# Layer norms cut into pieces, the two cell gates in one product, and the expert bias added on GpSimd, in a two-layer gated cross-attention kernel

## The chip, the cores and the metric

The kernel runs on one NeuronCore of one Trainium2 chip. A core has TensorE (PE) for matrix products, VectorE (DVE) and ScalarE (ACT) for work along rows, GpSimd (POOL) for other elementwise work, and SyncE (SP), which here only issues DMAs. [...] The metric is the device time of one execution in microseconds, the median of several runs.

## The reference

Eight sequences of 512 tokens with 256 features each (`x`) pass through two layers, with a context of the same shape. All numbers are float32. Cut to what matters:

```python
# layer 0: a gated linear cell (8 heads of 32) over the context
q = layernorm(x);  k = v = ctx
ifg = concat([q, k, v], axis=-1)              # 768 features; k and v are the same tensor
ig = ifg @ igate_w.T + igate_b;  fg = ifg @ fgate_w.T + fgate_b
cs = cumsum(log_sigmoid(fg));  log_D = causal(cs_s - cs_t + ig_t)
C = (q @ k.T / sqrt(32)) * exp(log_D - max(log_D))
h = (C / (max(|sum C|, exp(-max log_D)) + 1e-6)) @ v
x = x + tanh(g_xattn[0]) * layernorm(h) * ln_scale
# layer 0: self-attention with 32 heads of 8, then 8 experts of fixed token blocks
xn = layernorm(layernorm(x)) * ln_g + ln_b
o = softmax(q @ k.T / sqrt(8)) @ v @ wo + layernorm(x)
y = gelu(o_block @ w1[e] + b1[e]) @ w2[e] + b2[e]     # 256 tokens per expert and sequence
x = x + tanh(g_ffn[0]) * y
# layer 1: cross-attention with 16 heads of 16 and a key mask
x = x + tanh(g_xattn[1]) * (softmax(mask(layernorm(x) Wq . ctx Wk)) @ (ctx Wv) @ Wo + bo)
# layer 1: product-key memory of 4096 experts, top 8 of 8 heads
x = x + tanh(g_ffn[1]) * memory(layernorm(x))
```

Since `k` and `v` of the cell are the same context, a gate's weights on `k` and on `v` meet the same factors.

## The kernel before

The kernel has three stages. The first holds the cell, both attentions, the experts and most of the first product of the memory; a second folds the memory's batch norm into its keys; a third finds the top keys and adds up the memory's rows. The change touches the first stage only, so the other two are told no further.

Tokens lie on the 128 partitions in `NC` = 4 blocks, with 256 features along the row, where a layer norm is done; products need the features on the partitions, and `to_features` (L243) gets there by eight transposes on TensorE and two copies.

The first stage is written as a planner. An outer loop (L937) walks the softmax attentions, 24 jobs of 16 steps, with two half-ticks per step. In each half-tick it issues two score products for the row maxima of one job (`maxima`, L325) and two for the exponentials of the job before (`exponentials`, L353); after them come the maximum on VectorE (L333) and the exponential on ScalarE (L361), and in every second half-tick the products with the values (L376). Scores have two PSUM buffers for both kinds together, so the next pair of a kind waits until the last one was read. Then `beside` (L915) hands out side work for a credit of 1.3 or 2.4 units. Side work comes in five lanes, generators that issue a few instructions and then yield:

- a number is the cost of TensorE work just issued, taken from the credit;
- `("wait", t)` puts the lane to sleep until the planner's clock `now` has gone on by `t`. The clock moves at the end of a half-tick alone, by 2.6 units (`RETURN`) or by the work issued, if that is more;
- `("rest", event)` waits for another lane, and `("take", True)` for the one accumulator bank `ac` of PSUM.

The lane `before` (L843) runs `cell` (L440) and `queries` (L602) for each sequence `m`, `behind` runs `experts` (L645), `operands` (L712) and `values1`, `after` runs `leave` (L760), and `fill` runs `inner` (L798), products of the memory that fill what is left.

The order that comes out of this binds TensorE alone (`ORDERED`, L31). The other engines' queues are ordered by a scheduler, which takes instructions as it finds them ready, the earlier written first among equals, and which also sets the waits. DMAs in `load`, `load_context` and `load_expert` go through GpSimd's queue, nearly all others through SyncE's.

What the change touches:

- `layernorm` (L83): four statistics (L90), four aggregates (L92), the variance's power of -1/2 on GpSimd (L93, L94), four normalizations (L96). It is called for six norms per sequence: `qn` and `hk` in the cell, two in `queries`, one each in `operands` and `leave`. All its instructions are issued at once; the caller then waits, mostly 6.5 units.
- The gates of the cell (L457 to L472): for each of two gates six products of 8 output rows by 512 tokens (L463), two with the query's features and four with the context's, into `ac`, and an addition of the bias (L469).
- The end of the cell (L593 to L599): the norm of `hk`, its scale `lns` on VectorE (L594), and the addition to the freshly loaded `X` on GpSimd (L598).
- The experts (L668 to L707): after eight blocks of the first product (L674) and the Gelu (L685), the second product starts with a product of a row of ones with the bias row `b2e` (L689) and goes on with sixteen products (L696); the result, times `tanh(g)`, is added to `X` (L702). `load_expert` (L428) fetches `w1e`, `w2e` and `b2e` of the next expert, with one buffer each.

## Time and profile before

| what | value |
|---|---|
| median of 3 runs | 4510.04 us (4505.13 to 4513.51) |
| profiled execution | 4499.43 us, of which the span from first to last instruction 4497.7 us |
| mean granted TensorE clock | 0.915 |
| products of the gates (L463) | 192 records, 592 ns each (two records per product) |
| products of the bias (L689) | 32 records, 620 ns each (two per product) |
| norm: statistics, aggregate, normalization | 192 each; 410, 154 and 408 ns |
| norm: power on GpSimd (L93, L94) | 48 each; 227 and 1040 ns |
| scale of `hk` on VectorE (L594) | 8, 1221 ns |
| addition to `X` on GpSimd (L598) | 8, 2167 ns |
| `x2` on GpSimd (L656) | 32, 1219 ns |
| load of `b2e` | 16, 1 KB each, 1.7 us from issue to landing |

A record's duration is from its start to its modelled end; products overlap in TensorE's pipeline, so the spacing of two starts says what one costs. The profile names a line, an engine, an operation and its tiles; behind an arrow stands what ended the idle time ahead of it.

### The profile page before, as it was taken

To read this page: it belongs to the slowest core of one execution; us is meant where nothing else is said; L and a number is where in the kernel's file an instruction comes from. 1 tells how busy PE (TensorE), PEld (TensorE's weight loads), DVE (VectorE), ACT (ScalarE), POOL (GpSimd) and SP (SyncE) were. 2 spreads that over 40 slices of the span, in tenths; PEclk is the share of its full clock that TensorE was granted. 3 is DMA by queue.
4 is the path that set the end of the run, shared out by engine and by line. 5 is a ranking of instruction groups with operands and counts; after the bars stand their busy time and mean duration, and the time that the engine had idled before them with its cause. 6 is when DMAs were issued, how large, how long until landed. Compare 5 with 4: busy or idle time off the path is not lost.

```text
span 4497.7 us, 74502 instructions
## 1 busy us (share of the span) xinstructions
PE 3866.6 (86%) x30857; PEld 1939.2 (43%) x30857; DVE 2473.7 (55%) x5662; ACT 1586.7 (35%) x2035; POOL 563.0 (13%) x572
## 2 busy tenths in 40 slices
PE   6778797879988998998899898788997689999998
PEld 2222333433334333333334343233444366666667
DVE  3555534554454455455544534443200599999995
ACT  2124343334443543443344344442431122332331
POOL 3110101100011001001100100000000122222222
PEclk7679889999999999999999999998998689999999
DMA  3210112122213222222321231102345012222221
GB/s 95 46 38 25 39 43 64 50 60 84 64 51 96 79 60 71 86 60 74 80 84 60 74 110 37 44 23 62 102 134 119 25 67 91 88 86 89 91 89 42
DMA packets 191983, 312.73 MB, mean 70 GB/s; under 512 B 20430, under 2 KB 145902, under 8 KB 184238
## 3 DMA queue, kind: packets, MB, share of 16 engines
q1 hardware_dynamic: 173452, 239.98, 17.8%
q0 software_dynamic: 15520, 62.94, 5.0%
q10 hardware_dynamic: 2672, 5.04, 0.4%
q8 instruction: 243, 3.98, 0.4%
q14 instruction: 96, 0.79, 0.1%
HBM read 218.85 MB, written 88.24 MB: 68 GB/s over the span
## 4 chain that ended last, share of the span: by engine, by line
PE 62%; DVE 19%; DMA 3%; ACT 2%; issue 2%; POOL 1%; SPq 0%; DVEq 0%; POOLq 0%; ACTq 0%
PE sc L316 18%; PE acc L1272 9%; PE ps_hd L118 8%; DVE nm L333 7%; PE av L376 6%; PE ps_y L696 3%; PE ps_h L674 2%; PE ps_p L267 2%; PE ps_q L278 2%; PE ps_sim L1153 2%; PE cf L1254 1%; PE ps_hl L118 1%; DVE gs L1263 1%; DVE m L1241 1%; DVE m L1243 1%
## 5 line engine op out<-in xcount | busy, mean ns | idle before, releaser
L333 DVE TENSOR_REDUCE nm<-sc 128x2 f32<-128x1024 f32 x768 | 939.6, 1224 | 1114.0 <-PE sc L316 1112.3
L316 PE MATMUL sc<-ka,qa 32*128 32x512 f32 x3072 | 968.5, 688 | 284.3 <-DVE nm L333 256.2
L361 ACT ACTIVATE pr<-sc 128x1024 f32<-128x1024 f32 x768 | 785.1, 1023 | 1195.5 <-PE sc L316 1192.9
L316 PE MATMUL sc<-qa,ka 32*128 32x512 f32 x3072 | 925.5, 674 | 13.0 <-ACT pr L361 7.4
L316 PEld LDWEIGHTS sc<-ka,qa 32*128 32x128 f32 x3072 | 262.9, 195 | 716.9 <-DVE nm L333 501.4
L1272 PE MATMUL acc<-up_sb,gs 64*128 64x256 f32 x4096 | 495.3, 397 | 43.2 <-DVE gs L1263 43.2
L118 PE MATMUL ps_hd<-xT,dw 128*64 128x256 f32 x3584 | 435.0, 388 | 20.4 <-DVE pd L555 8.5
L1272 PEld LDWEIGHTS acc<-up_sb,gs 64*128 64x128 f32 x4096 | 409.0, 197 | 100.1 <-DVE gs L1263 45.3
L376 PE MATMUL av<-pr,v 128*32 128x512 f32 x3072 | 437.2, 643 | 5.5 <-ACT pr L361 5.5
L118 PEld LDWEIGHTS ps_hd<-xT,dw 128*64 128x64 f32 x3584 | 242.2, 138 | 253.9 <-issue 101.9
L1244 POOL TENSOR_TENSOR m<-m,chT 128x1024 f32<-128x1024 f32 x128 | 257.1, 2008 | 723.9 <-DVE m L1243 556.4
L316 PEld LDWEIGHTS sc<-qa,ka 32*128 32x128 f32 x3072 | 249.6, 192 | 63.8 <-issue 26.7
L814 ACT COPY hb<-ps_hd 128x512 f32<-128x512 f32 x224 | 131.0, 585 | 326.6 <-PE ps_hd L118 291.9
L376 PEld LDWEIGHTS av<-pr,v 128*32 128x32 f32 x3072 | 62.1, 111 | 320.9 <-issue 303.3
L528 ACT ACTIVATE pd<-mb,aT 128x512 f32<-128x512 f32 (+3 forms) x256 | 129.6, 553 | 176.0 <-PE cav L535 84.2
L520 POOL TENSOR_SCALAR_AFFINE_SELECT mb<-mb 128x256 f32<-128x256 f32 x128 | 52.1, 407 | 1111.4 <-ACT pd L528 520.5
L1254 PEld LDWEIGHTS cf<-m,m 64*64 64x64 f32 x8192 | 139.8, 142 | 91.6 <-issue 75.3
L1254 PE MATMUL cf<-m,m 64*64 64x64 f32 x8192 | 156.9, 229 | 23.4 <-DVE gs L1263 18.2
L1241 DVE TENSOR_TENSOR m<-chT,iota 128x1024 f32<-128x1024 f32 x128 | 170.6, 1332 | 2.0 <-ACT chT L1230 2.0
L555 DVE SCALAR_TENSOR_TENSOR pd<-csc,pd 128x512 f32<-128x512 f32 (+3 forms) x256 | 115.7, 485 | 92.0 <-PE csc L550 67.1
L1187 ACT ACT_TABLE_LOAD x28 | 35.9, 1283 | 360.8 <-DVE w L1186 341.9
L550 PE MATMUL csc<-qT,cT 32*128 32x256 f32 (+3 forms) x512 | 146.9, 554 | 17.1 <-DVE pd L555 13.2
(215 smaller groups left out, 4366.8 us busy)
## 6 DMA issues: line engine op xcount, KB each, us to landing
h_d<-hb SPq DMA_DIRECT2D x224, 256.0 KB
gs<-h_d SPq DMA_DIRECT2D x56, 1024.0 KB
dw<-in_down SPq DMA_DIRECT2D x112, 256.0 KB
w1e<-in_w POOLq DMA_DIRECT2D x16, 1024.0 KB, 5.4
w2e<-in_w POOLq DMA_DIRECT2D x16, 1024.0 KB, 6.5
mb<-nM_d SPq DMA_DIRECT2D x32, 512.0 KB
qk_d<-pk SPq DMA_DIRECT2D x64, 256.0 KB
ws<-in_w SPq DMA_DIRECT2D x56, 256.0 KB
```

The costliest lines, as they stand in the source:

```text
L118: nc.tensor.matmul(ps[64 * q : 64 * q + 64, :], dw[:, k, :], runs[:, :, q, :], start=(k == 0), stop=(k == NK - 1),)
L316: nc.tensor.matmul(sc[:, i, :], lhs[r : r + 32, g, c * P : (c + 1) * P], rhs[r : r + 32, g, :], start=True, stop=True,)
L333: nc.vector.tensor_reduce(self.nm[:, c, 2 * half : 2 * half + 2, g], sc, AX.X, ALU.max, negate=True)
L361: nc.scalar.activation(self.pr[jj], sc, AF.Exp)
L376: nc.tensor.matmul(self.av[32 * j : 32 * j + 32, :], self.va[:, c, h * (self.hd + 1) : h * (self.hd + 1) + 32], pr[j // 2][:, j % 2, :], s ...
L550: nc.tensor.matmul(sc[i][:, s0:], cT[r : r + 32, g, s0 : s0 + P], qT[r : r + 32, g, s0:], start=True, stop=True,)
L696: nc.tensor.matmul(py[:, c, :], hT[:, f, c * P : (c + 1) * P], w2e[:, f, :], start=False, stop=(f == NF - 1 and c == 1),)
L814: nc.scalar.copy(hb.rearrange("p n i t -> p i n t"), ps.rearrange("p i (n t) -> p i n t", n=2),)
L1241: nc.vector.tensor_tensor(m1, spread(0), grid, ALU.is_equal)
L1244: nc.gpsimd.tensor_tensor(m2, m2, spread(2), ALU.mult)
L1254: nc.tensor.matmul(cf[64 * q : 64 * q + 64, h, s, :], m2[rows, q, s, :], m1[rows, q, s, :], start=True, stop=True,)
L1272: nc.tensor.matmul(accs[n][q], gs[n % 2][rows, i, :], up_sb[rows, i, :], start=(i == 0), stop=(i == 63),)
```

## The change

Six edits, in the order of the code:

1. `layernorm` becomes a generator with four pieces. It yields after two statistics, after the power, and after each two normalizations, with waits of 1, 3, 1.5 and 1.5 units; callers use `yield from` and drop their own waits after it (in `queries` two, 5 and 6.5; in the cell, `operands` and `leave` 6.5 each). Its small tiles get tags by user.
2. At the start, the gates' weights are gathered in a tile `gwm` of 40 columns: one gate in columns 0 to 7, the other in 32 to 39, with the weights on `k` and `v` summed. Biases are loaded to the same rows. `gw_sb` and `m_f` move into the buffers of later tiles.
3. The cell's gates are one accumulation of four products with 40 output rows, from which both gates are read.
4. The scale of `hk` moves from VectorE to GpSimd, and the waits around the addition to `X` are changed from 6 and 2 units to one of 5 after it.
5. `b2e` is loaded broadcast to all partitions, scaled by `tanh(g)` on GpSimd, and added there to the expert's half of `X` before its products.
6. The expert's second product loses the bias product, and its sixteen products run with the token half outside and the feature block inside.

The diff, less the removed empty lines and the unchanged context:

```diff
...
     nc.sync.dma_start(tg, gates.partition_broadcast(P))
     nc.scalar.activation(tg, tg, AF.Tanh)
-    def layernorm(dst, src, keep=1):
-        st = small.tile([P, NC, 6], F32, name="ln_st")
-        mv = small.tile([P, NC, 2], F32, name="ln_mv", tag=f"ln_mv{keep}", bufs=keep + 1)
-        rs = small.tile([P, NC], F32, name="ln_rs", tag=f"ln_rs{keep}", bufs=keep + 1)
+    def layernorm(dst, src, user):
+        st = small.tile([P, NC, 6], F32, name="ln_st", tag=f"ln_st{user}", bufs=1)
+        mv = small.tile([P, NC, 2], F32, name="ln_mv", tag=f"ln_mv{user}", bufs=4 if user == "x" else 1)
+        rs = small.tile([P, NC], F32, name="ln_rs", tag=f"ln_rs{user}", bufs=4 if user == "x" else 1)
         for c in range(NC):
             nc.vector.bn_stats(st[:, c, :], src[:, c, :])
+            if c == 1:
+                yield ("wait", 1)
         for c in range(NC):
             nc.vector.bn_aggr(mv[:, c, :], st[:, c, :])
         nc.gpsimd.tensor_scalar(rs, mv[:, :, 1], EPS_LN, None, ALU.add)
         nc.gpsimd.tensor_tensor(rs, rs, mhalf.to_broadcast([P, NC]), ALU.pow)
+        yield ("wait", 3)
         for c in range(NC):
             nc.vector.tensor_scalar(
                 dst[:, c, :], src[:, c, :], mv[:, c, 0:1], rs[:, c : c + 1], ALU.subtract, ALU.mult
             )
+            if c % 2:
+                yield ("wait", 1.5)
         return mv, rs
...
         ps_m = ctx.enter_context(tc.tile_pool(name="ps_m", bufs=2, space=PSUM))
-        gw_sb = cst.tile([P, 6, 16], F32, name="gw_sb")
+        gw_sb = row.tile([P, 6, 16], F32, name="gw_sb", tag="cs")
         nc.sync.dma_start(gw_sb, gw.rearrange("(k p) n -> p k n", p=P))
-        gb_sb = cst.tile([8, 2], F32, name="gb_sb")
-        nc.sync.dma_start(gb_sb, gb)
+        gb_sb = cst.tile([40, 1], F32, name="gb_sb")
+        for i in range(2):
+            nc.sync.dma_start(gb_sb[32 * i : 32 * i + 8], gb[:, i : i + 1])
+        gwm = cst.tile([P, 4, 40], F32, name="gwm")
+        nc.gpsimd.memset(gwm, 0.0)
+        for i in range(2):
+            part = slice(8 * i, 8 * i + 8)
+            nc.vector.tensor_copy(gwm[:, 0:2, 32 * i : 32 * i + 8], gw_sb[:, 0:2, part])
+            nc.vector.tensor_tensor(
+                gwm[:, 2:4, 32 * i : 32 * i + 8], gw_sb[:, 2:4, part], gw_sb[:, 4:6, part], ALU.add
+            )
         class Weights:
...
         m_u8 = cst.tile([B * NC, P], U8, name="m_u8")
         nc.sync.dma_start(m_u8, mask)
-        m_f = cst.tile([B * NC, P], F32, name="m_f")
+        m_f = row.tile([B * NC, P], F32, name="m_f", tag="e")
         nc.vector.tensor_copy(m_f, m_u8)
         mp = ps_m.tile([P, S], F32, name="mp", tag="m")
         nc.tensor.transpose(mp[:, : B * NC], m_f, ident[: B * NC, : B * NC])
...
             nc.gpsimd.dma_start(w1e, w1[e].rearrange("(k p) f -> p k f", p=P))
             w2e = wmp.tile([P, NF, D], F32, name="w2e", tag="w2e")
             nc.gpsimd.dma_start(w2e, w2[e].rearrange("(f p) d -> p f d", p=P))
-            b2e = wmp.tile([1, D], F32, name="b2e", tag="b2e")
-            nc.gpsimd.dma_start(b2e, b2[e : e + 1])
+            b2e = wmp.tile([P, D], F32, name="b2e", tag="b2e")
+            nc.gpsimd.dma_start(b2e, b2[e].partition_broadcast(P))
             weights[n] = (e, w1e, w2e, b2e)
...
                     cx[b, c * P : (c + 1) * P].rearrange("p (h e) -> p h e", e=32),
                 )
             yield ("wait", 4)
-            layernorm(qn, qn)
-            yield ("wait", 6.5)
+            yield from layernorm(qn, qn, "q")
             qT = trp.tile([P, NK, S], F32, name="qT", tag="qT")
             yield from to_features(qT, qn)
+            yield ("take", True)
+            gp = ps_ac.tile([P, S], F32, name="gp", tag="ac")
+            for k in range(4):
+                if k:
+                    yield 0.9
+                nc.tensor.matmul(
+                    gp[:40], gwm[:, k, :], qT[:, k, :] if k < 2 else cT[:, k - 2, :],
+                    start=(k == 0), stop=(k == 3),
+                )
             gates = []
             for i in (1, 0):
-                yield ("take", True)
-                gp = ps_ac.tile([P, S], F32, name="gp", tag="ac")
-                for k in range(6):
-                    if k:
-                        yield 0.9
-                    nc.tensor.matmul(
-                        gp[:8], gw_sb[:, k, 8 * i : 8 * i + 8],
-                        qT[:, k, :] if k < 2 else cT[:, k % 2, :],
-                        start=(k == 0), stop=(k == 5),
-                    )
                 g = row.tile([8, S], F32, name="gate", tag=f"g{i}")
-                nc.vector.tensor_scalar(g, gp[:8], gb_sb[:, i : i + 1], None, ALU.add)
+                part = slice(32 * i, 32 * i + 8)
+                nc.vector.tensor_scalar(g, gp[part], gb_sb[part], None, ALU.add)
                 gates.append(g)
-                yield ("take", False)
-                yield 0.9
+            yield ("take", False)
+            yield 0.9
             z, a = gates
             e = row.tile([16, S], F32, name="e", tag="e")[:8]
...
             nc.scalar.activation(e, e, AF.Exp, scale=-1.0)
             nc.scalar.activation(e, e, AF.Ln, bias=1.0)
             nc.vector.scalar_tensor_tensor(z, z, 0.0, e, ALU.min, ALU.subtract)
-            cs = row.tile([8, S], F32, name="cs")
+            cs = row.tile([8, S], F32, name="cs", tag="cs")
             nc.vector.tensor_tensor_scan(
                 cs, ones[:8, 0:1].to_broadcast([8, S]), z, 0.0, ALU.mult, ALU.add
             )
...
                 yield 1.1
             yield ("rest", ("left", m - 3))
             Xb = load(m)
-            layernorm(hk, hk)
-            nc.vector.tensor_tensor(
+            yield from layernorm(hk, hk, "q")
+            nc.gpsimd.tensor_tensor(
                 hk, hk, lns.unsqueeze(1).to_broadcast([P, NC, D]), ALU.mult
             )
-            yield ("wait", 6)
             nc.gpsimd.tensor_tensor(Xb, Xb, hk, ALU.add)
-            yield ("wait", 2)
+            yield ("wait", 5)
         def queries(m):
             xn = tok.tile([P, NC, D], F32, name="xn", tag="t1")
-            lnx[m] = layernorm(xn, xbs[m][:, :, :D], keep=3)
-            yield ("wait", 5)
-            layernorm(xn, xn)
-            yield ("wait", 6.5)
+            lnx[m] = yield from layernorm(xn, xbs[m][:, :, :D], "x")
+            yield from layernorm(xn, xn, "q")
             yield ("rest", ("v0", m - 1))
             nT = nTs[m] = trp.tile([P, NK, S], F32, name="nT", tag="nT")
             yield from to_features(nT, xn, affine=True)
...
             yield from to_features(fT, x2)
             for i in range(2):
                 e, w1e, w2e, b2e = weights[2 * m + i]
+                xc = Xb[:, 2 * i : 2 * i + 2, :]
+                nc.gpsimd.tensor_scalar(b2e, b2e, tg[:, 1:2], None, ALU.mult)
+                nc.gpsimd.tensor_tensor(
+                    xc, xc, b2e.unsqueeze(1).to_broadcast([P, 2, D]), ALU.add
+                )
                 hT = wmp.tile([P, NF, D], F32, name="heT")
                 for f in range(NF):
                     ps = ps_m.tile([P, S], F32, name="ps_h", tag="m")
...
                 yield ("wait", 4)
                 yield ("take", True)
                 py = ps_ac.tile([P, 2, D], F32, name="ps_y", tag="ac")
-                nc.tensor.matmul(
-                    py, ones[0:1, :], b2e.unsqueeze(1).to_broadcast([1, 2, D]),
-                    start=True, stop=False,
-                )
-                yield 0.9
-                for f in range(NF):
-                    for c in range(2):
+                for c in range(2):
+                    for f in range(NF):
                         nc.tensor.matmul(
                             py[:, c, :], hT[:, f, c * P : (c + 1) * P], w2e[:, f, :],
-                            start=False, stop=(f == NF - 1 and c == 1),
+                            start=(f == 0), stop=(f == NF - 1),
                         )
-                    yield 0.9
-                xc = Xb[:, 2 * i : 2 * i + 2, :]
+                        if f % 2:
+                            yield 0.9
                 nc.vector.scalar_tensor_tensor(xc, py, tg[:, 1:2], xc, ALU.mult, ALU.add)
                 yield ("take", False)
                 if 2 * m + i + 1 < 16:
...
             Xb, cT = xbs[m][:, :, :D], cTs[m]
             b = order[m]
             xn = tok.tile([P, NC, D], F32, name="xn3", tag="t2")
-            layernorm(xn, Xb)
+            yield from layernorm(xn, Xb, "o")
             nc.gpsimd.tensor_tensor(Xb, Xb, tbo.unsqueeze(1).to_broadcast([P, NC, D]), ALU.add)
-            yield ("wait", 6.5)
             nT = trp.tile([P, NK, S], F32, name="nT3", tag="l2")
             yield from to_features(nT, xn)
             q1, k1 = cross_set(m)
...
                 yield 1.0
             nc.sync.dma_start(x_d[NC * b : NC * (b + 1)].rearrange("c p d -> p c d"), Xb)
             yield ("wait", 2)
-            layernorm(Xb, Xb)
-            yield ("wait", 6.5)
+            yield from layernorm(Xb, Xb, "l")
             xT4 = xTs[m] = exp.tile([P, NK, S], F32, name="xT4", tag="xT", bufs=1)
             yield from to_features(xT4, Xb)
             nc.sync.dma_start(xT_d[:, :, b * S : (b + 1) * S], xT4)
```

## The prediction

> **What bounds the kernel now.** I read the page first (busy time, the chain that ended last, the costliest groups), then the waits of TensorE, then its timeline in two places.
>
> ```profile
> PE 3866.6 (86%) x30857; PEld 1939.2 (43%) x30857; DVE 2473.7 (55%) x5662; ACT 1586.7 (35%) x2035; POOL 563.0 (13%) x572
> ...
> PE 62%; DVE 19%; DMA 3%; ACT 2%; issue 2%; POOL 1%; SPq 0%; DVEq 0%; POOLq 0%; ACTq 0%
> ...
> L333 DVE TENSOR_REDUCE nm<-sc 128x2 f32<-128x1024 f32 x768 | 939.6, 1224 | 1114.0 <-PE sc L316 1112.3
> L316 PE MATMUL sc<-ka,qa 32*128 32x512 f32 x3072 | 968.5, 688 | 284.3 <-DVE nm L333 256.2
> ```
>
> TensorE carries 62% of the chain. Of the rest, 19% is VectorE, and the group L333 shows where: the row maxima of the scores, 1.22 us each, whose end frees the score buffer for TensorE. The waits of TensorE in the whole span:
>
> ```profile
> PE sc L316 <- DVE nm L333: 261.5, 244, 6.9
> ...
> PE csc L550 <- DVE pd L555: 13.2, 6, 5.6
> ```
>
> One wait outweighs all others (us, times, longest). The change touches only the attention stage, which ends at about 3375 us; the two later stages stay as they are. That stage is a sequence of rounds: four score products, then side work of other steps, then the next four. Two places of its timeline, first without and then with gate products:
>
> ```profile
> 2900.16 0.69 PE L316 MATMUL sc<-ka,qa 32*128 32x512 f32 x1 [0.74 <-DVE nm L333]
> ...
> 2901.23 1.07 PE L376 MATMUL av<-pr,v 128*32 128x512 f32 x8
> 2902.63 0.69 PE L316 MATMUL sc<-ka,qa 32*128 32x512 f32 x1 [0.34 <-DVE nm L333]
> ...
> 2905.11 0.69 PE L316 MATMUL sc<-ka,qa 32*128 32x512 f32 x1 [1.33 <-DVE nm L333]
> ```
>
> ```profile
> 1060.21 0.69 PE L316 MATMUL sc<-ka,qa 32*128 32x512 f32 x1
> ...
> 1061.29 1.03 PE L463 MATMUL gp<-qT,gw_sb 128*8 128x512 f32 x2
> 1062.15 1.02 PE L463 MATMUL gp<-cT,gw_sb 128*8 128x512 f32 x2
> 1063.10 0.69 PE L316 MATMUL sc<-ka,qa 32*128 32x512 f32 x1
> ```
>
> And the product that adds an expert's bias, ahead of the expert's own:
>
> ```profile
> 814.48 1.08 PE L689 MATMUL ps_y<-b2e,ones 1*128 1x512 f32 x2
> 815.49 5.30 PE L696 MATMUL ps_y<-w2e,heT 128*128 128x256 f32 x16
> ```
>
> A round lasts 2.47 us (2900.16, 2902.63, 2905.11) whether 1.0 us of side work lies in it or none: the maximum's way through VectorE and back sets it. With two gate products it lasts 2.89 us (1060.21 to 1063.10), of which TensorE works all. So a round takes the longer of about 2.5 us and 1.14 us plus its side work. I walked all rounds of the trace that hold both kinds of score product, after 300 us: 239 with under 1.5 us of side work have medians of 2.5 us and hold 181 us of idle TensorE; the 462 with more hold 101 us, 5% of their time.
>
> **What the Trainium skill says.** "FP8 and Floating Point Precision", TensorE Precision Notes: true fp32 makes four passes; "TensorE: Matmul & The Clock Gate", Back-to-back issue gap: some 216 ns for a pass of 512 columns, set by the columns streamed, not by output rows. The trace agrees: four times 216 is 0.86, and a gate product has 1061.29 to 1062.15 = 0.86 us with 8 output rows. I take the same for 40. "SBUF — State Buffer", SBUF: two separate sides: VectorE in a two-port mode and GpSimd lock each other out for a whole instruction. The trace agrees: the norm pieces (L96, median 0.41 us) once took 2.28 us beside the 2.28 us add on GpSimd:
>
> ```profile
> 2535.93 4.54 DVE L96 TENSOR_SCALAR xn<-X,ln_mv,ln_rs 128x256 f32<-128x256 f32 x8 [0.52 <-POOL ln_rs L94]
> ```
> ```profile
> 2537.39 2.28 POOL L717 TENSOR_TENSOR X<-X,tbo 128x1024 f32<-128x1024 f32 x1 [0.36 <-DVE xn L96]
> ```
>
> "GPSIMD Engine Reference", Performance versus the Vector engine: an fp32 add of two tensors is 1.96 times as long on GpSimd. Here 1.22 us (L594, VectorE) stand against 2.17 us (L598, GpSimd) on 1024 columns, 1.78 times.
>
> **The change part by part.**
>
> *Gates.* Twelve products per cell become four: 8 cells x 8 x 0.86 = 55 us of TensorE work gone. *Expert bias.* One product for each of 16 experts goes; it holds TensorE 815.49 - 814.48 = 1.01 us, 16 us in sum. Together 71 us at full clock. The expert's own products change their order (token half outside, feature block inside), not their number or size; the first now needs both Gelu halves sooner, and a planned wait of 4 units lies ahead of it, so I cost it at nothing; uncovered it would be one Gelu of about 1 us an expert.
>
> How much shows depends on the rounds that it leaves. The planner writes TensorE's order, so the changed order can be counted without running it. I laid each product's spacing in this trace against both orders: side work falls from 1711 to 1641 us, but rounds of both kinds with under 1.5 us of it rise from 238 to 277 of some 700: no other step is ready to move in. Summing the longer of 2.5 us and 1.14 us plus side work over all rounds gives 2729 before and 2687 after, 42 us less; with a floor of 2.7 us, as the thin rounds' means are (2.7 to 3.1), 34 us. The planner's own clock is the pessimist: 2978.2 units in the old order, 2977.3 in the new, though 14.7 units of that are a later first round, which only its timers make; about 15 remain gained. I take -38, with -15 and -71 as ends.
>
> *Layer norms in four pieces.* TensorE alone keeps the written order; the other engines are ordered by a scheduler by readiness. In VectorE's built order the pieces are mostly back in a block (four statistics, four aggregates, four norms). Places with over 2 us of other VectorE work between two maxima are 66 before and 64 after, their excess 97 and 89 us by this trace's durations. TensorE's idle gaps overlap some 62 us of layer-norm work in the trace, so a tenth of that, with the moved scale (next), is -5; ends -20 and 0. The timers themselves (7 units in four waits in place of 6.5 in one, and the planner's clock moves only at half-ticks of 2.6 units or more) place transposes later in TensorE's order. In the old trace TensorE waits for a norm before transposes only in the start (16.8 and 19.5 us) and once for 4.0 us, so nothing is to be had there.
>
> *Scale of hk on GpSimd.* Eight times 1.22 us leave VectorE (4 us of them under TensorE's idle, counted above) and 2.17 us go to GpSimd. The add behind it (L598) is 0.95 us later.
>
> *Bias on GpSimd.* Per expert a scale of 256 columns (not shown; between 0.23 us of L93 and 1.22 us of L656, I take 1.0), an add of 512 columns (half of L598, 1.1), and a load of 128 KB in place of 1 KB: issue 0.53 us before, at most 0.94 (w2e's row), I take 0.8; landing between 1.7 us (now) and 3.6 us (cte's 128 KB), I take 3. In GpSimd's built order they stand right behind x2 (L656, 4.84 us): add, load, scale, add, load, scale, of which the scales wait for the landing, 1.1 + 0.8 + 3 + 1.0, twice, 12 us a layer. Queued behind are the load of the next X, its add of hk and the norms' powers. At 1357 us x2 ended 5.4 us before that load could go, so X comes some 6 us late there; the longer timers give more room than that before its transposes. The cell's masks (L520) stand further back in most layers; TensorE's waits on the cell are small now (13.2 us at csc). Port locks add: 16 x 2.1 + 8 x 2.2 = 51 us more of GpSimd. I charge +4, ends 0 and +30 (2 us per expert).
>
> *Start.* In cell 0 the first gate comes after four products instead of six, -2; the scale is +0.95; the second norm of queries(0) stands behind an add and a load more, +1.9; 128 KB more come in ahead of qn, +0.6. Sum +1.5.
>
> *The new sum of context weights*, one memset and four small VectorE operations, lies under the wait for qn (VectorE idle 12.0 us there); uncovered it would be 2 us.
>
> Sum: -38 - 5 + 4 + 1.5 = -37 us. The profiled execution took 4499.4 us (span 4497.7 and 1.7 around it), so 4462 by its measure; the runs' median, 4510.0, stands 10.6 above it, so I forecast 4510 - 37 = 4473.
>
> **The rivals.**
> - *All TensorE work removed comes through*, 71 us and some of the norms': 4510 - 71 = 4439, reckoned as 4430 to 4455. For it: the gate rounds of cells 1 to 7 have nearly no idle. Against: 1 us less in a 2.89 us round gives 0.4. Chance 0.13.
> - *The floor swallows it*: rounds stay as many (some 700 with both products), and the planner's clock stands still. Time within 9 us of 4510. Measurement can tell about 0.2%, 9 us, from no change. Chance 0.14.
> - *GpSimd's queue becomes the wait* (slower): the scale behind a landing bias holds the powers, the next X and the masks, and locks VectorE. The price is what TensorE loses per expert; without my +4 the sum is -41.5, so at 41.5/16 = 2.6 us it ends level and beyond 3.2 us slower; at 4 us (-41.5 + 64) it is 4532, at 5 us 4548. For it: in the old trace GpSimd's waits for w1e and w2e already delayed a norm's power by 8 us (1751 to 1759). Against: TensorE hardly waited then. Chance 0.12.
> - Mine, 4455 to 4500, 0.61.
>
> **How the numbers follow.** Faster by over 0.2% is my case and the first rival, 0.74; within, 0.14; slower, 0.12. The range leaves out the fastest tenth and the slowest: 4440 to 4522. My case alone is 4455 to 4500.
>
> **What would show it.** TensorE busy some 65 to 80 us less; L316's idle behind L333 up by 20 to 40 us from 256; L463's group down to 64 records of the same 0.59 us; layer norms still blocks on VectorE; the first score round within 3 us of 166.4. I am wrong if TensorE's waits for transposes of xn or for csc grow past 20 us, if GpSimd appears in the chain above 1%, or if the 40-row product is longer than 0.86 us.

## The result, and the profile after

The changed kernel takes 4437.32 us in the median (4423.54 to 4447.40) beside 4507.59 for the kernel before on the same chip: 0.984 of its time, with a 95% interval of 0.9813 to 0.9867. That is 70 us less, where 37 were forecast; the time lies just under the low end of the range, 4440. A second comparison gave 4440.83 and 0.983 (0.9804 to 0.9855).

The page of the changed kernel: busy times, the chain, the maxima and the score products behind them.

```profile
PE 3779.7 (85%) x30697; PEld 1922.5 (43%) x30697; DVE 2473.8 (56%) x5662; ACT 1580.1 (36%) x2029; POOL 616.8 (14%) x613
...
PE 37%; DVE 17%; DMA 3%; ACT 1%; issue 1%; POOL 1%; SPq 0%; DVEq 0%; POOLq 0%; ACTq 0%
...
L348 DVE TENSOR_REDUCE nm<-sc 128x2 f32<-128x1024 f32 x768 | 939.1, 1224 | 1047.0 <-PE sc L331 1043.2
L331 PE MATMUL sc<-ka,qa 32*128 32x512 f32 x3072 | 960.7, 684 | 297.4 <-DVE nm L348 284.4
```

TensorE is busy 87 us less, where 65 to 80 were forecast, and its idle time behind the maxima rises by 28 us (256.2 before), as forecast. The shares of the chain can't be set beside those before: they are shares of the whole span, and the chain is followed back from the end to 1742 us here, to 476 us before. What TensorE waited for, us, times and longest:

```profile
PE sc L331 <- DVE nm L348: 285.3, 286, 12.0
...
PE csc L564 <- DVE pd L569: 7.2, 3, 4.5
```

One of the signs that the forecast named for its being wrong is there: TensorE waits 23.0 us for `xn` ahead of transposes, past the 20 named. It is a single wait in the start, which was 19.5 us before.

The gates, in TensorE's timeline: two products with 40 output rows (two records each) take 1.84 us to the next score product, where two with 8 rows took 1.81 (1061.29 to 1063.10). Of the Trainium skill, "TensorE: Matmul & The Clock Gate", Back-to-back issue gap, the forecast used some 216 ns for 512 columns; the same section gives 131 ns for a sustained stream. The 0.86 us of a product here, 215 ns for each of four passes, decides for the first.

```profile
1086.49 1.91 PE L475 MATMUL gp<-qT,gwm 128*40 128x512 f32 x4
1088.33 0.69 PE L331 MATMUL sc<-ka,qa 32*128 32x512 f32 x1
```

So far the trace looks like the forecast. What it doesn't show is where 70 us come from. I split the attention stage, from the first score product to the last product of the memory, into TensorE's work reckoned at full clock (the time in which any product is under way, by its record), what it lost because the clock was granted at half (the records of the clock in this stage are 0.5 or 1.0), and idle time. Idle time I split by what held TensorE: a maximum with norm work ahead of it on VectorE since the maximum before; one with over 1.2 us of other work ahead of it; one with neither; a score product for the maxima that waited for something else than a maximum (mostly transfers of `qa` and `ka`); and all gaps ahead of other products. Two of the experiments below stand beside it; each row is one profiled execution (us):

| kernel | stage | work | clock | idle | norm ahead | other ahead | neither | operands | other gaps |
|---|---|---|---|---|---|---|---|---|---|
| before | 3205.8 | 2613.4 | 187.8 | 404.6 | 114.8 | 29.0 | 113.3 | 22.4 | 125.2 |
| whole change | 3139.0 | 2544.1 | 177.3 | 417.6 | 113.6 | 32.6 | 138.7 | 7.6 | 125.1 |
| gates and bias | 3194.9 | 2553.6 | 183.2 | 458.1 | 131.0 | 21.1 | 138.2 | 24.1 | 143.7 |
| waits alone | 3158.3 | 2612.8 | 177.2 | 368.3 | 114.6 | 23.8 | 110.1 | 6.7 | 113.1 |

In the whole change 69 us of work and 11 of clock loss are gone, and idle time is up by only 13. The column "norm ahead" hardly moves: as a whole, the norms hold the maxima as long as before.

### The profile page after: what moved, and what is told of

Its sections match the earlier page's. It is cut to its first block, busy times and chain, and to the rows that moved or that the text cites. A ratio compares the mean times of both kernels' runs of the same rounds, so it can differ in the third digit from the quotient of the medians.

```text
span 4436.9 us, 74250 instructions
## 1 busy us (share of the span) xinstructions
PE 3779.7 (85%) x30697; PEld 1922.5 (43%) x30697; DVE 2473.8 (56%) x5662; ACT 1580.1 (36%) x2029; POOL 616.8 (14%) x613
## 4 chain that ended last, share of the span: by engine, by line
PE 37%; DVE 17%; DMA 3%; ACT 1%; issue 1%; POOL 1%; SPq 0%; DVEq 0%; POOLq 0%; ACTq 0%
PE sc L331 10%; PE acc L1281 7%; PE ps_hd L123 6%; DVE nm L348 4%; PE av L391 3%; DVE m L1250 2%; DVE gs L1272 2%; DVE m L1252 2%; PE ps_y L707 1%; PE ps_hl L123 1%; DVE i L1176 1%; PE ps_h L690 1%; PE ps_sim L1162 1%; PE ps_q L293 1%; PE cf L1263 1%
```

## The experiments

**The granted clock.** One thing first, since it decides how the numbers are read. In all comparisons together the kernel before took 4479.29 to 4533.86 us, at a mean granted clock of 0.920 down to 0.908 in the single runs. Time and clock go together (correlation -0.88): 4.1 us for a thousandth of clock. The trace of the kernel before gives about as much: 188 us lost in 443 us at half clock is 0.42 us each, and a thousandth of the mean clock is 9 us more at half clock in 4500, an estimate of 3.8 us. The last column of the table takes each kernel's median to a clock of 0.913 with this slope, and gives its distance from the kernel before at that clock, 4508 us. It is worked out, not measured, and where a kernel's own order moves the clock it takes away a part of its effect; but it makes the parts comparable.

| run | edits | ratio to before (95%) | median, us | less than before, us | mean clock | at clock 0.913 |
|---|---|---|---|---|---|---|
| e1 | 2, 3 | 0.997 (0.9955-0.9986) | 4491.44 | 13 | 0.9121 | -20 |
| e2 | 5, 6 | 0.9896 (0.9859-0.9932) | 4462.31 | 42 | 0.9188 | -22 |
| e3 | 2, 3, 5, 6 | 0.9962 (0.9948-0.9976) | 4486.83 | 17 | 0.9126 | -23 |
| e4 | 2, 3 in place | 0.9946 (0.992-0.9972) | 4482.14 | 22 | 0.9091 | -42 |
| e5 | 1, 4 | 0.9856 (0.9837-0.9874) | 4447.04 | 68 | 0.9180 | -40 |
| e6 | 1, 4, 5, 6 | 0.9838 (0.9815-0.9862) | 4443.94 | 71 | 0.9178 | -44 |
| e7 | all but 4 | 0.9819 (0.9804-0.9833) | 4432.02 | 83 | 0.9128 | -77 |
| e8 | 2, 3, 5, 6, scale of 4 | 0.9952 (0.9934-0.997) | 4495.35 | 19 | 0.9106 | -22 |
| e9 | e5, norms in one block | 0.9849 (0.982-0.9878) | 4453.73 | 62 | 0.9176 | -35 |
| e10 | e5, short waits | 0.9883 (0.9851-0.9916) | 4468.77 | 47 | 0.9148 | -32 |
| e13 | buffers of 1 | 0.9981 (0.9967-0.9994) | 4505.55 | 8 | 0.9120 | -6 |
| e14 | e5, old buffers | 0.9908 (0.9882-0.9934) | 4471.72 | 41 | 0.9137 | -33 |
| e15 | e3, buffers of 1 | 0.9953 (0.9937-0.9968) | 4493.38 | 20 | 0.9105 | -25 |
| e16 | waits of 1 | 0.9868 (0.9841-0.9895) | 4451.05 | 60 | 0.9178 | -37 |
| e17 | another wait | 0.9957 (0.9936-0.9977) | 4493.16 | 18 | 0.9142 | -10 |
| e18 | another wait | 1.0003 (0.9988-1.0018) | 4511.01 | 0 | 0.9115 | -3 |
| e11 | 1, 5, 6, and e4 | 0.9791 (0.9766-0.9815) | 4419.34 | 97 | 0.9124 | -91 |
| e12 | whole change | 0.983 (0.9804-0.9855) | 4440.83 | 75 | 0.9138 | -64 |

The first comparison of the whole change (clock 0.9158) stands at -59 in the last column.

### Gates and bias

Gates alone (e1) and bias alone (e2) are those edits of the change and nothing else:

```diff
-                for k in range(6):
+            for k in range(4):
...
                 nc.tensor.matmul(
-                        gp[:8], gw_sb[:, k, 8 * i : 8 * i + 8],
+                    gp[:40], gwm[:, k, :], qT[:, k, :] if k < 2 else cT[:, k - 2, :],
```
```diff
-                nc.tensor.matmul(
-                    py, ones[0:1, :], b2e.unsqueeze(1).to_broadcast([1, 2, D]),
-                    start=True, stop=False,
-                )
...
+                nc.gpsimd.tensor_tensor(
+                    xc, xc, b2e.unsqueeze(1).to_broadcast([P, 2, D]), ALU.add
+                )
```

> The kernel before with the two cell gates in one product of 40 columns (and the gathered weights), nothing else. Theory WORK (what TensorE no longer does comes off at the spacing it had at the granted clock: 64 products of 0.96 us = 61 us, less a few us of new idle): -50 to -61 us. Theory FLOOR (the prediction's sum: a round lasts the longer of 2.5 us and its work; this kernel's order has 262 thin rounds instead of 237 and a sum 27 us smaller): -20 to -33 us. Theory NORMS (most of the gain comes from the norms in pieces): under -25 us.

> The kernel before with the expert bias added on GpSimd and the bias product gone, nothing else. WORK: 16 products of 1.2 us spacing at the granted clock = -19 us. FLOOR: -16 us. If GpSimd's longer queue costs something: 0 or slower.

e3 makes both. e4 merges the gates as e1 does, but the planner is charged as if the old twelve products were still issued, so that fewer other steps move up:

```diff
             for i in (1, 0):
                 for k in range(6):
                     if k:
                         yield 0.9
+                    if i and k < 4:
+                        nc.tensor.matmul(gp[:40], gwm[:, k, :], ...)
```

> The kernel before with gates in one product and bias on GpSimd, norms and the scale of hk as before. WORK: -68 to -80 us, the whole change's gain or more. FLOOR: -36 us (order: 264 thin rounds). NORMS: about half of the change's 70 us, the rest belonging to the pieces.

> The gates in one product, but the planner is told the old costs, so that every other TensorE instruction stands where it stood in the kernel before and nothing is moved into the emptied rounds. WORK: -50 to -61 us all the same. FLOOR: -32 us by its count (259 thin rounds), since emptied rounds stop at 2.5 us. If the planner's refilling is what brought the gain, this one is clearly slower than the first kernel of this set.

The gates give 13 us for 44.5 us of work gone from the stage, gates and bias 17 for 60. TensorE's waits in e3 show where the rest went (261.5 us in 244 waits before):

```profile
PE sc L326 <- DVE nm L343: 295.9, 271, 12.4
...
PE ps_q L288 <- DVE v L763: 12.6, 5, 4.5
```

In the table of idle times, "neither" rises by 25 us: rounds whose side work was taken out and which now only wait for the maximum's way through VectorE. That is the floor, as forecast. But "norm ahead" and "other gaps" rise by 16 and 18 as well, which the floor doesn't have. Of 60 us, 54 became idle time. WORK is out, and FLOOR (-36) was too generous. e4 tells more of it: it is left with as much work in the stage as e1 (2568.3 and 2568.8 us), but its idle time is 412.3 us, only 8 above the kernel before, where e1 has 438.0, in a profiled execution 20 us above its median. This points to the steps that moved up as the source of most of the new idle time, not to the products that went; one execution of each shows no more. What e4 saves there it loses at half clock, 212.0 us in place of 187.8; its mean clock is the lowest of the table. Why it is so low was not tested.

The bias, at -42, gave more than the work that it removes; at one clock it is 22. Its trace has 12 us less work in the stage, 10 less idle time and 15 less lost at half clock. The two together are no sum of the two apart: at one clock -23 against -20 and -22.

### Norms, and the scale of hk

e5 is edits 1 and 4 alone. e6 adds the bias, e7 is the whole change with the scale of `hk` left on VectorE and its old waits, and e8 is e3 with the scale of `hk` on GpSimd:

```diff
-            nc.vector.tensor_tensor(
+            nc.gpsimd.tensor_tensor(
                 hk, hk, lns.unsqueeze(1).to_broadcast([P, NC, D]), ALU.mult
             )
             yield ("wait", 6)
```

> Edits 1 and 4 alone: layer norms in pieces with their four waits, the scale of hk on GpSimd; the old gates and the old expert bias. Built TensorE order: 232 of the thin rounds (237 before), side work 1705 us (1711). Theory NORMS (the pieces keep VectorE free for the maxima and are what the gates and the bias lacked): -35 to -55 us, TensorE's idle time behind the maxima down by 20 us or more, clock loss as before. Theory FLOOR (only the count of the rounds matters): -10 us. Theory ORDER (pieces and timers only move steps; what is gained depends on which rounds come out full, and is worth no fixed sum): within 15 us of the kernel before.

> Edits 1, 4, 5 and 6: everything but the gates (2 and 3). Built order: 252 thin rounds, side work 1689 us. NORMS: the bias alone gave -42, with the norms' -35 to -55 it is -75 to -95, faster than the whole change, since the gates give next to nothing. FLOOR: -16. ORDER: -30 to -50, no more than the bias alone, and the whole change's -70 needs the gates too.

> The whole change without edit 4's scale: the scale of hk stays on VectorE, and the old waits of 6 and 2 units around the addition to X stay; the norm of hk is in pieces. Built order: 268 thin rounds, side work 1641 us, floor sum 2686 us as in the whole change (2687). NORMS: as the whole change, -65 to -75 (the scale is 8 instructions of 1.22 us on VectorE, under 10 us in all). FLOOR: -43. ORDER: anywhere between gates and bias alone (-17) and the whole change (-70), as the order differs from both.

> Gates and bias (2, 3, 5, 6) with the scale of hk on GpSimd, and the old waits: TensorE's built order is that of gates and bias alone, instruction for instruction; VectorE loses eight instructions of 1.22 us. All theories: -17 us as gates and bias alone gave, or up to 10 us better; if it comes to -40 or more, the scale on VectorE was what cost the missing time (theory HK: it stands ahead of maxima at a place where the cell's chain is late).

The edit forecast at -5 gives 68 us by the medians (65 by the ratio, which the later expectations quote), about as much as the whole change; at one clock it is 40. So the 70 us come from here, in large part. It isn't the scale: e7 has the gain without it, and e8, with it, hasn't. The scale on GpSimd rather costs: the add to `X` stands behind it, and the next norm on VectorE waits for that add. VectorE's waits, before and then after:

```profile
DVE ln_st L90 <- DMA qn<-in_x: 33.9, 8, 12.0
...
DVE ln_st L90 <- POOL X L598: 28.0, 8, 6.4
```
```profile
DVE ln_st L90 <- POOL X L611: 48.1, 8, 11.4
...
DVE ln_st L90 <- DMA qn<-in_x: 37.1, 8, 13.8
```

28.0 became 48.1 us. The scale has a part of that: in e8, where it moves alone, 30.1 us (e3) became 37.9, 1.0 us for each of 8. Most of the rest is two waits, in the fifth and the seventh cell, of 11.4 and 11.1 us, where the kernel before has 4.6 and 4.8; and these come from the bias. GpSimd, then VectorE, then TensorE at the first of them:

```profile
1336.15 1.27 POOL L683 TENSOR_TENSOR X<-X,b2e 128x512 f32<-128x512 f32 x1
...
1348.07 0.91 POOL L682 TENSOR_SCALAR b2e<-b2e,tg 128x256 f32<-128x256 f32 x1 [2.68 <-DMA b2e<-in_b]
1348.94 0.82 POOL L434 DMA_DIRECT2D X<-in_x  x1
```
```profile
1355.44 1.40 DVE L90 BATCH_NORM_STATS2 ln_st<-X 128x6 f32<-128x256 f32 x4 [11.42 <-POOL X L611]
```
```profile
1360.86 1.22 PE L331 MATMUL sc<-ka,qa 32*128 32x512 f32 x1 [11.99 <-DVE nm L348]
```

From 1336.15 to 1348.98 us GpSimd works off the rows of two experts, add, load, scale, add, load, scale, and waits twice for a row to land. Only then does it issue the load of the next `X`. The norm of that `X` is the next instruction on VectorE, with a maximum behind it, and TensorE stands idle for 11.99 us; at the second place it is 11.63. Waits of 11 us or more for this `X` are in every trace that has both the bias on GpSimd and the new waits (two in the whole change, both times, and one each in e6, e7 and e11), and in none that has only one of the two.

In e7 VectorE's wait for `X` is 34.3 us in all. The intervals of e7 and of the whole change overlap, so that e7 is faster is not shown.

### Which part of the norms' edit

The edit has three parts: the instructions are issued in pieces, the waits behind them are others, and the small tiles have buffers by user. Three kernels take e5 apart. e9 issues a norm at once and puts the four waits behind it; e10 keeps the pieces with short waits; e14 keeps pieces and waits with the old tags:

```diff
-            if c == 1:
-                yield ("wait", 1)
...
+        yield ("wait", 1)
+        yield ("wait", 3)
+        yield ("wait", 1.5)
+        yield ("wait", 1.5)
```
```diff
             if c == 1:
-                yield ("wait", 1)
+                yield ("wait", 0.1)
...
-        yield ("wait", 3)
+        yield ("wait", 0.1)
...
-            if c % 2:
-                yield ("wait", 1.5)
+            if c == 1:
+                yield ("wait", 0.1)
```
```diff
-        st = small.tile([P, NC, 6], F32, name="ln_st", tag=f"ln_st{user}", bufs=1)
-        mv = small.tile([P, NC, 2], F32, name="ln_mv", tag=f"ln_mv{user}", bufs=4 if user == "x" else 1)
...
+        keep = 3 if user == "x" else 1
+        st = small.tile([P, NC, 6], F32, name="ln_st")
+        mv = small.tile([P, NC, 2], F32, name="ln_mv", tag=f"ln_mv{keep}", bufs=keep + 1)
...
```

> The run of edits 1 and 4 alone (-65), with one difference: all instructions of a norm are issued at once, and the four waits (1, 3, 1.5, 1.5 units) follow behind them. The planner's clock, and so the place of every later step in TensorE's order, is as in that run; the written order on VectorE differs in 24 of some 3182 rows, since the scheduler had put most of the pieces back into blocks. Theory DELAY (what counts is that the four waits end one or two half-ticks later than one of 6.5, so that the steps behind a norm stand later in TensorE's order): -60 to -70. Theory PIECES (what counts is that the pieces are issued between other work): the gain goes, -20 to 0.

> The run of edits 1 and 4 alone (-65), with the pieces kept but their waits made as short as the planner can: 0.1 units behind two statistics, behind the power and behind two normalizations, none behind the last, so that a norm takes three half-ticks as it did before, where the four waits take four to five. Built order: 229 thin rounds, side work 1711 us. DELAY: the gain goes, within 15 us of the kernel before or slower, and TensorE waits for qn, xn or X ahead of transposes by some 10 us more. PIECES: -40 to -65 stays.

The pieces add nothing that can be told: 62 us less without them, 68 with. But short waits keep 47, so each theory missed one of the two. That left the buffers, or the order of TensorE's work as such. e13 is the kernel before with the new tags and nothing else, e15 is e3 with them:

```diff
-        st = small.tile([P, NC, 6], F32, name="ln_st")
-        mv = small.tile([P, NC, 2], F32, name="ln_mv", tag=f"ln_mv{keep}", bufs=keep + 1)
+        st = small.tile([P, NC, 6], F32, name="ln_st", tag=f"ln_st{user}", bufs=1)
+        mv = small.tile([P, NC, 2], F32, name="ln_mv", tag=f"ln_mv{user}", bufs=4 if user == "x" else 1)
...
```

> The kernel before with nothing but the small tiles of the norms changed: ln_st, ln_mv and ln_rs get the tags by user (x, q, o, l) that the change gives them, in place of tags that nearly all norms share; no pieces, no other waits, no other edit. TensorE's written order is that of the kernel before, instruction for instruction; VectorE's differs in some 50 places: the norm of hk stands earlier, out of the block that it formed with the norm of X. Theory BUFFERS (norms that shared two buffers were held back until an earlier norm had ended, and then fell on VectorE in one block ahead of a maximum): -40 to -60, idle time of TensorE behind the maxima in rounds with much side work down by 20 us or more. Theory ORDER (any other order of TensorE was better than the old one by chance): within 10 us of the kernel before.

> Edits 1 and 4 alone (-65) with the old tags of ln_st, ln_mv and ln_rs: pieces, waits and the scale of hk as in the change. TensorE's written order is that of edits 1 and 4 alone. BUFFERS: most of the gain goes, -20 to 0. ORDER: -50 to -65 stays.

> Gates and bias (2, 3, 5, 6; -17) with the tags by user alone; no pieces, old waits, the scale of hk on VectorE. TensorE's written order is that of gates and bias. BUFFERS: -60 to -75, as much as the whole change. ORDER: -17 as before.

The buffers are worth 8 us alone, and nothing that can be told beside gates and bias. With the old buffers 41 us of e5's 68 stay; the intervals lie apart, but at one clock only 7 us are between them. BUFFERS as the main cause is out; a part of it beside the new waits isn't. e16 then changes nothing but the waits behind the six norms in the kernel before; e17 and e18 change one wait each that has nothing to do with the change:

```diff
             layernorm(qn, qn)
-            yield ("wait", 6.5)
+            yield ("wait", 1)
+            yield ("wait", 3)
+            yield ("wait", 1.5)
+            yield ("wait", 1.5)
```
```diff
                 if i == 0:
-                    yield ("wait", 20)
+                    yield ("wait", 16)
```
```diff
-            yield ("wait", 2)
+            yield ("wait", 3)
             layernorm(Xb, Xb)
```

> The kernel before with the waits behind the six norms changed and nothing else: four waits (1, 3, 1.5, 1.5 units) in place of one of 6.5 (of 5 behind the first norm in queries), and the same four behind the norm of hk, which had none. Norms in one block, old buffers, scale of hk on VectorE. Built order: 816 rounds, 244 thin, side work 1705 us, floor sum 2718.5 (2728.9 before). Theory WAITS (the planner's waits, through TensorE's order, carry what edits 1 and 4 gave with the old buffers): -30 to -45. If the pieces or the scale of hk are needed for it: -15 to 0.

> The kernel before with one wait changed that has nothing to do with norms, gates or the bias: between the two experts of a sequence, 16 units in place of 20. TensorE's written order then differs in 971 lines of some 6700 (1574 for edits 1 and 4, about 1100 for the pieces with short waits). Built order: 814 rounds, 225 thin, side work 1711 us, floor sum 2719 us. Theory ANY ORDER (the old order was a bad draw, and most others are better): -20 to -50. Theory WAITS (what helps is that the steps behind a norm come later): within 10 us of the kernel before. FLOOR: -10.

> The kernel before with the wait ahead of the last norm of a sequence (in leave, behind the store of X) 3 units in place of 2. TensorE's written order differs in 942 lines. Built order: 819 rounds, 238 thin, side work 1707 us, floor sum 2724 us. ANY ORDER: -20 to -50. WAITS: within 10 us of the kernel before. FLOOR: -5.

The page of e16, its busy times, chain (followed back to 1353 us) and the score products behind the maxima:

```profile
PE 3857.5 (87%) x30857; PEld 1936.7 (43%) x30857; DVE 2488.5 (56%) x5667; ACT 1578.6 (35%) x2028; POOL 563.9 (13%) x572
...
PE 46%; DVE 17%; DMA 3%; ACT 1%; issue 1%; POOL 1%; DVEq 0%; POOLq 0%; SPq 0%; ACTq 0%
...
L316 PE MATMUL sc<-ka,qa 32*128 32x512 f32 x3072 | 959.5, 685 | 260.0 <-DVE nm L333 247.7
```

The waits alone give 60 us: constants of the planner at six places, with no instruction added or taken away. They act through the order in which the planner writes its steps. TensorE keeps that order and the other queues are built from it; the run doesn't tell the two apart. At one clock it is 37 us, and the trace of e16 has about the same: idle time of the stage is down by 36, and the idle time ahead of these products by 24 (284.3 before); 11 us less are lost at half clock besides. What the score products for the maxima waited for, other than maxima, in the kernel before and then in e16:

```profile
PE sc L316 <- DMA qa<-qk_d: 11.0, 2, 10.6
...
PE sc L316 <- issue: 5.5, 2, 3.1
...
PE sc L316 <- DMA ka<-qk_d: 4.8, 1, 4.8
PE sc L316 <- DMA dw<-in_down: 4.8, 1, 4.8
```

```profile
PE sc L316 <- DMA ka<-qk_d: 4.8, 1, 4.8
...
PE sc L316 <- issue: 3.9, 2, 3.7
...
PE sc L316 <- DMA qa<-nm_sb: 3.6, 3, 2.5
...
PE sc L316 <- DMA qa<-zero_d: 2.5, 1, 2.5
```

The gain doesn't lie where the edit was aimed at. "Norm ahead" is 114.6 us after 114.8, though the steps behind a norm now stand a half-tick or two later. It lies in the column of operands, 15.7 us, in the gaps ahead of other products, 12.1, and in maxima behind other work, 5.2. Of the operands, 10.6 us are a single wait for `qa` near 3077 us. It recurs, 10.2 to 10.7 us long, in every trace with the old waits and in e10, with the short ones, and is in none with the four new ones. Two other orders, some 950 lines away from the old one where short waits are 1099 and the whole of edits 1 and 4 1574, gave -18 and 0. So not any order is better. But e17 gave 18 us without touching a norm (10 at one clock), where WAITS allowed 10, and two draws are few: that the old order was an unlucky one is not excluded. Not tried were one longer wait in place of the four, and each of the six places alone; the norm of `hk` had no wait of its own before, so that e16 also lengthens the cell. Why just these orders meet fewer late operands stays open.

### A version that beats both

e11 is edits 1, 2, 5 and 6 with the gates merged as in e4 and the scale of `hk` left on VectorE; e12 is the whole change once more beside it.

> A version that may beat both: edits 1, 2, 5 and 6, the gates merged in place (one accumulation of four products, the planner charged as for the old twelve), and the scale of hk left on VectorE with its old waits. Built order: 808 rounds, 262 of them thin, floor sum 2673 us (2687 for the whole change). If the parts add up as the floor has it: 14 us under the whole change, -80 to -95. If a lower granted clock takes it back, as it did with the gates in place alone (0.909 against 0.913): -60 to -75, no different from the whole change.

> The whole change once more, beside the other three on one chip. All theories: -65 to -75, as in its first comparison (-70).

The waits of TensorE and the group of the score products in e11:

```profile
PE sc L331 <- DVE nm L348: 249.6, 264, 12.4
```
```profile
L331 PE MATMUL sc<-ka,qa 32*128 32x512 f32 x3072 | 976.6, 691 | 267.8 <-DVE nm L348 249.6
```

Behind the maxima TensorE stands 36 us less than in the whole change (285.3). e11 takes 4419.34 us against 4440.83 on the same chip, 21 us less. Its TensorE work in the stage is that of the whole change (2544.9 against 2544.1 us), and its idle time 383.4 us against 417.6. Two things set it apart from the whole change, the scale and the planner's charge. Against e7, which differs in the charge alone (measured on another chip, each against the kernel before there), it is 0.9791 to 0.9819 with intervals that overlap a little, 14 us at one clock, and its idle time is 383.4 us to 412.3; e4 and e1 stand alike, 22 us apart at one clock. This points to the charge: while the planner reckons with the old products, the other steps stay where they were, and less idle time comes in, as in e4. It isn't shown beyond that.

## Why the prediction was wrong, point by point

- **TensorE's work removed: right, the near match in part by luck.** 71 us forecast, 69 gone from the stage. Some 64 of the 71 lie in the stage, since the gates of the first cell stand ahead of it, and gates and bias alone took 60 out of it (e3). Edits 1 and 4 alone, which take no product away, show 6 us less too.
- **What of it shows: right mechanism, too large.** -38 forecast. Gates and bias alone gave 17 us, 23 at one clock. In the changed kernel the rounds with under 1.5 us of side work went from 239 to 291, beyond the 277 counted, and the idle time in "neither" rose by 25 us. The sum over rounds took the longer of floor and work for each. It left out the idle time that comes in at other places, 16 and 18 us in "norm ahead" and "other gaps" in e3, and the granted clock: in e4, where fewer steps move, idle time rose by 8 us and the loss at half clock by 24.
- **The norms, -5: the step that failed.** It was right that the pieces come out as blocks and do little (e9). Wrong was the sentence on the timers: "so nothing is to be had there". I looked only at what waited for norms, and found no wait to shorten. But a wait moves every step behind it, and lets others move up, and that order was worth 60 us by the medians and 37 at one clock (e16). In the forecast it was the count of rounds that should have seen it: 2718.5 against 2728.9 us, about a fourth of the 37. That count has no transfers of operands in it.
- **The scale of hk on GpSimd, inside the -5: not seen on its own** (e8: 19 us less, beside 17). It takes 2.34 us on GpSimd, where 2.17 were taken over from the add. The 0.95 us that the add would be later are 1.0 us of wait on VectorE for each cell in e8.
- **The bias on GpSimd, +4: right mechanism, too small.** GpSimd waits as forecast for the broadcast rows to land, and no engine waits for the bias's own two instructions:

```profile
L683 POOL TENSOR_TENSOR X<-X,b2e 128x512 f32<-128x512 f32 x16 | 18.9, 1180 | 0.7
...
L682 POOL TENSOR_SCALAR b2e<-b2e,tg 128x256 f32<-128x256 f32 x16 | 14.8, 925 | 53.4 <-DMA b2e<-in_b 53.3
```

 The estimates of 1.0 and 1.1 us stand at 0.93 and 1.18; the landing takes 4.1 us, where 3 was taken. But the load of the next `X` stands behind, as the forecast had it ("X comes some 6 us late there"), and the room that it saw in the longer timers was not enough: two of eight cells have VectorE wait 13 us more in sum than before, and TensorE stand 12.0 and 11.6 us. An estimate of the cost is thus some 13 us, within the ends of 0 and +30. Gates and bias with the old waits don't have it (e3). POOL stays at 1% of the chain, so the sign named for this didn't tell of it; that it would decide the whole, the slower rival, was rightly held small.
- **The start, +1.5:** the first score product came 2.4 us later, at 156.2 us in place of 153.8.
- **The rivals.** "All work comes through" has the time right (4430 to 4455) by luck, since the cause is wrong: 17 us of it come through, and the norms' waits made up the rest. Parts at one clock: gates and bias -23, waits -37, buffers -6, together -66; the whole change has -59 and -64. By the medians the same parts are 17, 60 and 8, together 85, where the whole change has 70 and 75, so that they add up only with the clock reckoned out.

The prediction weighed the edits by the work that they move. The waits inside the first one, a handful of numbers, gave more than any other part.

## What to carry to other kernels

In a kernel whose order comes out of a planner, a changed wait is an edit of its own: try it alone, with no other edit, before the gain is booked to the work around it. Work taken from the bounding engine shows only where that work was the longest thing in its round; what moves up in its place can cost as much as what went. Work given to an idle engine stands ahead of the loads in that engine's queue: in this kernel the bias cost its time there, and not where its own result was awaited. And read the time of a part against the granted clock of its runs before calling a few tenths of a per cent an effect.

## What the runs showed of the hardware

Executions of the same program differed by 1.2% (4479 to 4534 us), and the longer ones had the lower granted clock (0.920 to 0.908). The Trainium skill, "TensorE: Matmul & The Clock Gate", Part 1: The HAM clock gate, says that the clock is passed at a ratio of one half or in full, depending on how busy TensorE has been lately. The traces agree in the two ratios: the stage before has 0.5 in 443 us of 3206 and 1.0 in the rest. In the changed kernel a norm shows how a stall can cost twice. VectorE first, TensorE second:

```profile
537.12 1.41 DVE L90 BATCH_NORM_STATS2 ln_st<-qn 128x6 f32<-128x256 f32 x4 [2.17 <-DMA qn<-in_x]
...
540.75 1.38 DVE L99 TENSOR_SCALAR qn<-qn,ln_mv,ln_rs 128x256 f32<-128x256 f32 x4 [1.55 <-POOL ln_rs L96]
542.05 1.22 DVE L348 TENSOR_REDUCE nm<-sc 128x2 f32<-128x1024 f32 x1
```
```profile
536.19 0.59 PE L331 MATMUL sc<-ka,qa 32*128 32x512 f32 x1
...
543.71 1.86 PE L690 MATMUL ps_h<-fT,w1e 128*128 128x256 f32 x4 [3.42 <-DVE heT L695]
545.50 1.22 PE L331 MATMUL sc<-ka,qa 32*128 32x512 f32 x1
```

VectorE stands in its queue for the load of `qn` (2.17 us) and for the power on GpSimd (1.55 us), with the maximum behind it. TensorE is idle for 3.42 us until `heT` comes, which stands behind that maximum, and then its products run at half speed: 1.22 us in place of 0.69. The clock's record has 0.5 from 544.0 us on, for 3.4 us; the page gives 3413 ns as the window over which the activity is watched. These waits, 33.9 us for the load and 28.2, 13.5 and 12.7 us for the powers in the kernel before, add up to 88 us of VectorE, beside the 115 us of TensorE in "norm ahead". In the other kernels here they are 85 to 97 us, so none made them much shorter. An earlier load of `qn` wasn't tried.
